# Fewer picked columns on ScalarE, addresses loaded behind each operation, window sums placed ahead of the edge network

## The chip, the core and the metric

The kernel runs on one core of a Trainium2 chip. The core has a matrix engine (TensorE, PE in the profile; its weight loads are shown apart as PEld), a vector engine (VectorE, DVE), an activation engine (ScalarE, ACT), GpSimd (POOL) and a queue engine (SyncE, SP) that here only starts DMA transfers. Each engine executes its own instruction stream in order; they wait for one another through semaphores. The metric is the device time of one execution in microseconds; the median of several runs is compared.

## What is computed

One layer of a graph network on 12,500 nodes with 128 features and 412,500 edges, sorted by destination. The 128 features are 32 scalars and 32 vectors of three components. For each edge:

```python
h   = gelu(gelu(edge_attr_8 @ W_mlp1 / sqrt(8)) @ W_mlp2 / sqrt(64))
w00, w01, w10, w11 = h @ Wp_00, h @ Wp_01, h @ Wp_10, h @ Wp_11
e0, e1 = feat0[src], feat1[src]            # rows gathered at the edge's source node
mid0 = [w00*e0*a0,  w11*sum(e1*a1)/sqrt3]  # a0, a1: edge_attr_4
mid1 = [w01*e0*a1,  w10*e1*a0]
n0, n1 = segment_sum(mid0, dst), segment_sum(mid1, dst)
```

The sums go through two small matrices, are mixed with a linear map of the node itself, and the result plus the input x is normalised over its 128 features. `feat0, feat1` are x times a 128x128 matrix `wf`.

## The kernel before, in words

**Tiling.** A run is 512 consecutive edges (128 partitions x Q = 4 columns). There are 806 runs, handled two at a time: NP = 403 pairs, the trips of the main loop (`for p in range(NP)`, unrolled). Two pairs make a chunk of four runs: the pair with k = 0 is called the even pair here, that with k = 1 the odd pair. A first phase (some 190 us) turns x into the transposed copy `xT` that stays in SBUF, and into a table of features in DRAM.

**Where an edge's features come from.** For a run, 4 x 128 rows of 512 bytes are needed in the tile `G`. There are three ways to get a quarter of a run (128 rows):

- GpSimd gathers it from the table by an indirect DMA (`gather`, line 223 of the profile), about 18 runs ahead, into one of ten buffers.
- SP copies the rows of every fourteenth run one by one with plain DMAs whose addresses it reads from a list (`aid`, line 208).
- VectorE or ScalarE picks it: it copies 128 columns of `xT` one at a time into a tile `gt` (lines 188 and 192), each from an address held in a register; TensorE then multiplies the tile by `wf` (line 197) and ScalarE copies the product into `G` (line 198, `picked_rows`). The registers are filled by an instruction that loads addresses from an SBUF list (line 174). A quarter that is picked isn't gathered.

How many columns are picked in a pair, and where between other operations, is set by the table `SLOTS`: on ScalarE four slots a pair, 12, 16, 16 and 12 columns, from pair FROM = 6 on. With 397 pairs that fills 171 tiles of 128.

**The order within a pair.** The order of each engine's instructions is the order in which the loop body emits them (a manual schedule); buffers and semaphores alone decide when one may start. In the loop body, for pair p of chunk c:

1. gather for a later pair (POOL), loads of edges (SP).
2. even pair: VectorE makes `pl` (`placing`, L683) and `oh` (`hot_rows`, L624), both of which read constants kept in the PSUM tile `bank`.
3. TensorE sums the messages of pair p-1 into windows of nodes (`segments`, L670, tile `seg`); ScalarE copies the window to SBUF (`segments_kept`, L676, tile `sg`) within slot 0.
4. `picked_rows`; odd pair: `radial` (transposes edge attributes for a chunk ahead, L543/L545).
5. ScalarE slot 1; TensorE `weights(p+1)` (L597).
6. the edge network two chunks ahead: in the even pair `mlp1` (L554) with its two gelus (`gelu1`, L559), in the odd pair `mlp2` (L570) with `gelu2` (L576). The gelus stand within ScalarE's slots 2 and 3.
7. even pair: ScalarE copies edge attributes into `bank` (`show`, L632), between the two gelus.
8. even pair: TensorE adds the four window sums of the chunk before to one PSUM tile at offsets read from registers (`place`: a zeroing matmul L693 and eight matmul passes L697), which is again `bank`.
9. VectorE: three operations of `messages` (L650, L654 twice) with its own slots of picked columns between them; in the odd pair `select` (L639, tile `S`), which reads `bank`, and `add` (L710), which adds the placed sums to the accumulator `acc`.

`bank` is one PSUM tile with three uses: the placed sums, the shown attributes, and the constants. The framework that sets the waits orders accesses to a tile by the order in which the loop body emits them.

**A slot with an operation.** `picks` loads part of the slot's addresses ahead of the operation (`fetch(e, n // 8 * 4)`: 4 of 12, 8 of 16), issues the operation, loads the rest, and copies all columns of the slot.

Of the kernel before, what the change touches and what calls it, by code (L numbers as in the profile page):

```python
# [8 lines left out]
F32 = mybir.dt.float32  # L9
# [6 lines left out]
ACT = mybir.EngineType.Activation  # L16
DVE = mybir.EngineType.DVE
# [4 lines left out]
P = 128  # L22
# [7 lines left out]
CH = 4  # L30
PR = 2
# [14 lines left out]
AID_FROM = 36  # L46
AID_LEAD = 16
STEPS = 12
SLOTS = {DVE: ((24, 20, 20), (24, 16, 28)), ACT: ((12, 16, 16, 12), (12, 16, 16, 12))}
FROM = {DVE: 6, ACT: 6}  # L50
COL_Q = {DVE: Q - 2, ACT: Q - 3}
A_OF = (1, 2, 3, 0)
# [5 lines left out]
def gnn_kernel(ctx: ExitStack, tc: tile.TileContext, x, src, dst, ea4, ea8, w1_0, w1_1, wm1, wm2,  # L58
# [33 lines left out]
    x_bytes = xT.bitcast(U8)  # L92
    x_bytes = bass.AP(tensor=x_bytes.tensor, offset=x_bytes.offset - x_at, ap=[[4 * N, P], [1, x_at + 4 * N]])
# [18 lines left out]

    per_chunk = {e: sum(map(sum, slots)) for e, slots in SLOTS.items()}
    picked = {}
    for e, slots in SLOTS.items():
        picked[e], done = [], 0
# [46 lines left out]

    taken = {e: 0 for e in picked}

    def fetch(e, n):

        at = taken[e]
        n = min(n, len(picked[e]) * P - at)
        if n <= 0:  # L170
            return []
        taken[e] += n
        row, c0 = divmod(at, per_chunk[e])
        _, r = nc.values_load_multi_w_load_instructions(  # L174
            pick_rows[e, row // P][row % P:row % P + 1, c0:c0 + n], engines=[e], min_val=x_at,
            max_val=x_at + 4 * (N - 1), skip_runtime_bounds_check_because="addresses of columns")
        return [(at + k, r[k]) for k in range(n)]

    def copy_columns(e, columns):

        for at, r in columns:
            i, j = divmod(at, P)
            if j == 0:
                GT[e, i] = wk.tile([P, P], F32, name=f"gt{list(picked).index(e)}", bufs=3)
            to = GT[e, i][:, j:j + 1]
            col = x_bytes[:, bass.ds(r.with_bounds(guaranteed_mod_val=0, out_of_modulus=4), 4)].bitcast(F32)
            if e == DVE:
                nc.vector.tensor_copy(to, col)  # L188
                if waiting and j % 2:
                    waiting.pop(0)()  # L190
            else:
                nc.scalar.activation(to, col, AF.Copy)  # L192
# [192 lines left out]
    for b in range(NG):  # L385
        c = math.ceil((min((b + 1) * GN, N) + MARGIN) / N * NCH) - 1
# [202 lines left out]
    def weights(p):  # L589

        c, k = divmod(p, CH // PR)
        runs = [i for i in range(PR) if p * PR + i < NS]
        WP[p] = ps.tile([P, PR, Q, P], F32, name="w")
        for q in range(Q):
            for i in runs:
                rows = slice(i * HID, (i + 1) * HID)
                nc.tensor.matmul(WP[p][:, i, q, :], H2[c][q % 2][rows, k, q // 2, :], wpb[rows, :],  # L597
                                 start=True, stop=True)
# [29 lines left out]
    def show(c):  # L628

        n = min(CH, NS - c * CH)  # L630
        t0 = c * CH % ET * Q
        nc.scalar.activation(shown[:, :, :n * Q], e4[c * CH // ET][:, :, t0:t0 + n * Q], AF.Copy)  # L632
# [40 lines left out]
    def segments_kept(p):  # L673
        c, r = divmod(p * PR, CH)
        n = min(PR, NS - p * PR)
        nc.scalar.activation(SG[c][:, r:r + n, :], SEG[c][:, r:r + n, :], AF.Copy)  # L676
# [9 lines left out]
    def place(c):  # L686
        ns = min(CH, NS - c * CH)
        b, r = divmod(c, P)
        _, at = nc.values_load_multi_w_load_instructions(
            run_first[b][r:r + 1, :], engines=[PE], min_val=0, max_val=4 * (SPAN - W),  # L690
            skip_runtime_bounds_check_because="bounded above")
        ST[c] = pt = bank[:, :4 * SPAN].rearrange("p (a n) -> p a n", a=4)
        nc.tensor.matmul(pt.rearrange("p a n -> p (a n)"), none[:, :P], none, start=True, stop=False)  # L693
        to = pt.bitcast(U8)
        for k in range(ns):
            k_at = at[k].with_bounds(guaranteed_mod_val=0, out_of_modulus=4)
            nc.tensor.matmul(to[:, :, bass.ds(k_at, 4 * W)].bitcast(F32), SG[c][:, k, :],  # L697
                             PL[c][:, k, :].rearrange("p (a n) -> p a n", a=4), start=False, stop=k == ns - 1)
# [54 lines left out]
    waiting = []  # L753
# [188 lines left out]
    with tc.manual_schedule(engines={PE, ACT, DVE, SP}):  # L942
# [54 lines left out]
        clearing = []  # L997
        placed = added = 0

        def picks(e, p, i, op=None):  # L1000
            if p < FROM[e]:
                if op:
                    op()
                return
            n = SLOTS[e][p % (CH // PR)][i]
            if not op:
                copy_columns(e, fetch(e, n))
                return
            first = fetch(e, n // 8 * 4)
            op()  # L1010
            copy_columns(e, first + fetch(e, n - n // 8 * 4))

        for p in range(NP):
            c, k = divmod(p, CH // PR)
            mine = [s for s in range(p * PR, (p + 1) * PR) if s < NS]
            if p:
                for s in mine:
                    if s + LEAD - PR < NS:
                        gather(s + LEAD - PR)
            if k == 1 and c + EDGES_AHEAD < NCH:  # L1020
                load_edges(c + EDGES_AHEAD)
            for s in mine:
                if s % P == P // 2 - 16 and (s // P + 1) * P < NS:
                    load_raws(s // P + 1)
                if s % P == P // 2 and (s // P + 1) * P < NS:
                    load_indices(s // P + 1)
                if s % ET == 8 and s - 8 + ET < NS:
                    load_attributes(s // ET + 1)
                for t in range(P // ROWS):
                    a = s + AID_LEAD - t * STEPS // (P // ROWS)  # L1030
                    if a in aided:
                        aid(a, t)
            nets = c + 2 < NCH
            if k == 0:
                placing(c)
                if c + 1 < NCH:
                    hot_rows(c + 1)
            if p:
                segments(p - 1)
                picks(ACT, p, 0, lambda: segments_kept(p - 1))  # L1040
            for e in picked:
                for s in mine:
                    if (e, s + 2 * PR) in pick_of:
                        picked_rows(e, pick_of[e, s + 2 * PR])
            if k == 1 and c + 3 < NCH:
                radial(c + 3)
            cleared = bool(late)
            rest = list(kept)
            norm_kept()
            picks(ACT, p, 1)  # L1050
            if p + 1 < NP:
                weights(p + 1)
            if nets:
                (mlp1, mlp2)[k](c + 2)
                picks(ACT, p, 2, lambda: (gelu1, gelu2)[k](c + 2, 0))
            else:
                picks(ACT, p, 2)
            if k == 0 and c + 1 < NCH:
                show(c + 1)
            for s in mine:  # L1060
                if s % ET == 20 and s - 20 + ET < NS:
                    turn_attributes(s // ET + 1)
            if nets:
                picks(ACT, p, 3, lambda: (gelu1, gelu2)[k](c + 2, 1))
            else:
                picks(ACT, p, 3)
            if k == 0 and c > 0:
                place(c - 1)
                placed = c
            raws_next = [s + PR for s in mine if s + PR < raw_runs]  # L1070
            for s in raws_next:
                turn_rows(s)
            messages(p, 0)
            if k == 0:
                picks(DVE, p, 0)
            messages(p, 1)
            picks(DVE, p, 1 - k)
            for s in raws_next:
                features(s)
            if rest:  # L1080
                norm_rest()
            if cleared:
                new_sums()
                clearing += list(range(4))
            elif clearing:
                clear_sums(clearing.pop(0))
            if k == 1 and c + 1 < NCH:
                select(c + 1)
            if k == 1:
                picks(DVE, p, 1)  # L1090
            messages(p, 2)
            if k == 1 and placed > added:
                add(added)
                added += 1
            picks(DVE, p, 2)
            if k == 0 and 0 < added == c - 1:
                norm(due.get(added - 1, []))
            if p == 0:
                addresses()
                find_first()  # L1100
                new_sums()
                clearing = list(range(4))
            if p == NP - 4:
                count_odd()
# [52 lines left out]
```

## Time and profile before

| what | value |
|---|---|
| median of 3 runs | 5994.51 us (5955.32 to 5994.96) |
| the profiled execution | 5962.68 us, span 5960.8 us |
| instructions | 141,936 |
| busy share of the span: PE, PEld | 57 %, 44 % |
| DVE, ACT, POOL | 56 %, 52 %, 44 % |
| clock granted to TensorE, mean | 0.65 of full speed |
| DMA | 40 GB/s, busy 1 to 2 tenths |

Busy counts neither the loading of registers nor the issuing of DMAs. All five engines lie between 44 and 57 percent, so no share names the limit; the idle time and what ends it has to be read. "Idle before" in a group of instructions is the time in which the engine stood still just before one of the group; behind the arrow stands what ended most of it, "issue" where the profile shows no cause and "remote" where it shows no instruction that did it.

### The profile page before, as it was taken

What the parts mean: (1) busy time and instruction counts of PE and PEld (TensorE: products, weight loads), DVE (VectorE), ACT (ScalarE), POOL (GpSimd) and SP (SyncE); (2) the same over time, 40 slices, a digit from 0 to 9 for tenths busy, and PEclk for the clock granted to TensorE, in tenths of its full rate; (3) what the DMA queues carried; (4) which work ended last, traced back from release to release, by engine and by line L of the source; (5) the groups of instructions that cost most, each with busy time, mean ns of one, the idle gap of its engine ahead of it and who ended that gap; (6) DMA issues with size and microseconds to landing.
All of it is one profiled execution on the core that took longest, in us unless ns stands there. A gap on an engine that the chain in (4) does not pass through costs nothing. (4 is left out here: it accounts for less than half of the span.)

```text
span 5960.8 us, 141936 instructions
## 1 busy us (share of the span) xinstructions
PE 3407.7 (57%) x30231; PEld 2603.1 (44%) x30231; DVE 3366.2 (56%) x28706; ACT 3093.4 (52%) x24111; POOL 2636.3 (44%) x2801
## 2 busy tenths in 40 slices
PE   3665655556555555555556555556655555655556
PEld 2544444444444444444444444444434444443444
DVE  1265656555655555656555665566565555665556
ACT  0254555555555555555555555555554555555554
POOL 4344444444444444444444444444444444444441
PEclk5766666666666666666666666666666666666666
DMA  4211111111111111111111111111111111111111
GB/s 100 59 36 40 39 35 38 41 35 43 42 35 39 39 37 43 40 35 36 36 41 37 40 43 38 37 40 40 41 40 35 35 38 38 40 40 34 40 33 23
DMA packets 576979, 239.04 MB, mean 40 GB/s; under 512 B 481402, under 2 KB 526570, under 8 KB 576106
## 3 DMA queue, kind: packets, MB, share of 16 engines
q0 software_dynamic: 89408, 183.29, 10.8%
q1 hardware_dynamic: 465928, 40.14, 5.4%
q10 hardware_dynamic: 20770, 6.47, 0.5%
q14 instruction: 629, 5.15, 0.3%
q8 instruction: 244, 4.00, 0.3%
HBM read 216.86 MB, written 12.99 MB: 39 GB/s over the span
## 5 line engine op out<-in xcount | busy, mean ns | idle before, releaser
L223 POOL DMA_INDIRECT G<-table,idx x2722 | 2567.2, 943 | 3208.9 <-issue 1313.3
L192 ACT ACTIVATE gt<-xT 128x1 f32 x21888 | 2329.1, 189 | 924.5 <-issue 889.3
L188 DVE COPY gt<-xT 128x1 f32 x25984 | 1891.8, 145 | 1565.0 <-issue 1520.5
L670 PE MATMUL seg<-M,S 128*32 128x128 f32 x12896 | 845.7, 371 | 444.2 <-issue 426.8
L597 PE MATMUL w<-wpb,h 64*128 64x128 f32 x6448 | 855.1, 388 | 383.7 <-issue 383.1
L597 PEld LDWEIGHTS w<-wpb,h 64*128 64x128 f32 x6448 | 699.0, 277 | 554.6 <-issue 544.1
L670 PEld LDWEIGHTS seg<-M,S 128*32 128x32 f32 x12896 | 544.3, 148 | 692.1 <-issue 643.3
L654 DVE TENSOR_TENSOR M<-w,G 128x768 f32<-128x768 f32 x806 | 761.1, 945 | 2.7 <-issue 2.7
L676 ACT ACTIVATE sg<-seg 128x256 f32<-128x256 f32 x403 | 151.1, 375 | 1112.3 <-remote 777.6
L697 PEld LDWEIGHTS m<-pl,sg 128*128 128x128 f32 x1612 | 348.6, 312 | 797.7 <-issue 797.7
L693 PE MATMUL m<-none 128*128 128x384 bf16 x202 | 90.8, 450 | 786.1 <-ACT m L632 412.6
L554 PE MATMUL h<-eT,w1b 64*128 64x128 f32 x3232 | 439.3, 403 | 125.8 <-ACT G L198 95.9
L576 ACT ACTIVATE h<-h 128x512 f32<-128x512 f32 x404 | 237.1, 589 | 491.9 <-remote 377.0
L554 PEld LDWEIGHTS h<-eT,w1b 64*128 64x128 f32 x3232 | 394.3, 303 | 159.5 <-ACT G L198 120.5
L570 PE MATMUL h<-h,w2b 64*64 64x256 f32 x3232 | 393.5, 556 | 105.7 <-ACT G L198 68.7
L197 PE MATMUL h<-wf,gt 128*128 128x128 f32 x748 | 244.0, 411 | 268.2 <-issue 154.2
L650 DVE TENSOR_TENSOR M<-w,G 128x512 f32<-128x512 f32 x403 | 275.5, 684 | 204.1 <-remote 73.9
L697 PE MATMUL m<-pl,sg 128*128 128x128 f32 x1612 | 367.5, 404 | 0.0
L197 PEld LDWEIGHTS h<-wf,gt 128*128 128x128 f32 x748 | 162.8, 263 | 403.6 <-issue 246.9
L639 DVE TENSOR_TENSOR S<-oh,m 128x512 f32<-128x512 f32 x202 | 137.2, 679 | 356.7 <-PE m L697 251.4
L559 ACT ACTIVATE h<-h 128x512 f32<-128x512 f32 x404 | 234.6, 581 | 91.0 <-remote 37.9
L570 PEld LDWEIGHTS h<-h,w2b 64*64 64x64 f32 x3232 | 187.5, 186 | 214.9 <-ACT G L198 87.3
(123 smaller groups left out, 1592.5 us busy)
## 6 DMA issues: line engine op xcount, KB each, us to landing
G<-table SPq DMA_DIRECT2D x7040, 0.5 KB
G<-table,idx POOLq DMA_INDIRECT x2722
e<-in_edge_attr SPq DMA_DIRECT2D x201, 64.0 KB
xt<-in_x SPq DMA_DIRECT2D x24, 256.0 KB
table<-ft ACTq DMA_DIRECT2D x24, 256.0 KB
xt<-in_edge_attr SPq DMA_DIRECT2D x24, 256.0 KB
out<-y SPq DMA_DIRECT2D x24, 256.0 KB
xt<-in_dst SPq DMA_DIRECT2D x5, 256.0 KB
```

The source lines that it names most:

```text
L188: nc.vector.tensor_copy(to, col)
L192: nc.scalar.activation(to, col, AF.Copy)
L197: nc.tensor.matmul(pt, GT.pop((e, i)), wf, start=True, stop=True)
L223: nc.gpsimd.indirect_dma_start(out=G[s][:, q, :], out_offset=None, in_=x if s < raw_runs else table, in_offset=bass.IndirectOffsetOnAxis(a ...
L554: nc.tensor.matmul(p1[h][:, j // 2, j % 2, :], w1b[rows, j, :], eT[c][rows, :], start=True, stop=True)
L570: nc.tensor.matmul(p2[r][k * HID:(k + 1) * HID, h * n:(h + 1) * n], w2b[rows, :], H1[c][h][rows, k * n:(k + 1) * n], start=True, stop=True)
L576: nc.scalar.activation(H2[c][r].rearrange("p k j e -> p (k j e)"), P2[c][r], AF.Gelu_apprx_tanh, scale=1.0 / math.sqrt(HID))
L597: nc.tensor.matmul(WP[p][:, i, q, :], H2[c][q % 2][rows, k, q // 2, :], wpb[rows, :], start=True, stop=True)
L650: nc.vector.tensor_tensor(m[:, :, :, :MUL], w[:, :, :2 * MUL].rearrange("p q (a u) -> p q a u", a=2), g[:, :, None, :MUL].to_broadcast([P, ...
L654: nc.vector.tensor_tensor(m[:, :, j, MUL:].rearrange("p q (i u) -> p q i u", i=3), w[:, :, None, (2 + j) * MUL:(3 + j) * MUL].to_broadcast ...
L670: nc.tensor.matmul(SEG[c][q * W:(q + 1) * W, r + i, :], own[:, (r + i) * Q + q, h * W:(h + 1) * W], M[p][:, i, q, h, :], start=h == 0, sto ...
L697: nc.tensor.matmul(to[:, :, bass.ds(k_at, 4 * W)].bitcast(F32), SG[c][:, k, :], PL[c][:, k, :].rearrange("p (a n) -> p a n", a=4), start=F ...
```

## The change

Three things change, all within the main loop:

- ScalarE's slots become 12, 12, 12 and 8 columns (44 a pair in place of 56). What ScalarE no longer picks is gathered by GpSimd.
- A slot's addresses are loaded at once, with one instruction, behind the operation in front of it. `fetch` and `copy_columns` become one function, `pick`; `segments_kept` and the gelus stand ahead of the slot whose middle they were in. The second gelu now stands ahead of `turn_attributes`.
- `place` moves from the end of TensorE's even pair to between `weights(p+1)` and `mlp1`, so ahead of `show` too. Lines behind the first edit have numbers four lower in the changed kernel (L670 becomes L666).

VectorE's slots stay; only where the small steps of the normalisation are put between its columns follows a column's place in the slot rather than in the tile.

```diff
-SLOTS = {DVE: ((24, 20, 20), (24, 16, 28)), ACT: ((12, 16, 16, 12), (12, 16, 16, 12))}
+SLOTS = {DVE: ((24, 20, 20), (24, 16, 28)), ACT: ((12, 12, 12, 8), (12, 12, 12, 8))}
...
-    def fetch(e, n):
+    def pick(e, n):
...
-        return [(at + k, r[k]) for k in range(n)]
-
-    def copy_columns(e, columns):
-
-        for at, r in columns:
-            i, j = divmod(at, P)
+        for k in range(n):
+            i, j = divmod(at + k, P)
...
-                if waiting and j % 2:
+                if waiting and k % 2:
                     waiting.pop(0)()
...
-        def picks(e, p, i, op=None):
-            if p < FROM[e]:
-                if op:
-                    op()
-                return
-            n = SLOTS[e][p % (CH // PR)][i]
-            if not op:
-                copy_columns(e, fetch(e, n))
-                return
-            first = fetch(e, n // 8 * 4)
-            op()
-            copy_columns(e, first + fetch(e, n - n // 8 * 4))
+        def picks(e, p, i):
+            if p >= FROM[e]:
+                pick(e, SLOTS[e][p % (CH // PR)][i])
...
             if p:
                 segments(p - 1)
-                picks(ACT, p, 0, lambda: segments_kept(p - 1))
+                segments_kept(p - 1)
+            picks(ACT, p, 0)
...
             picks(ACT, p, 1)
             if p + 1 < NP:
                 weights(p + 1)
+            if k == 0 and c > 0:
+                place(c - 1)
+                placed = c
             if nets:
                 (mlp1, mlp2)[k](c + 2)
-                picks(ACT, p, 2, lambda: (gelu1, gelu2)[k](c + 2, 0))
-            else:
-                picks(ACT, p, 2)
+                (gelu1, gelu2)[k](c + 2, 0)
+            picks(ACT, p, 2)
             if k == 0 and c + 1 < NCH:
                 show(c + 1)
+            if nets:
+                (gelu1, gelu2)[k](c + 2, 1)
             for s in mine:
                 if s % ET == 20 and s - 20 + ET < NS:
                     turn_attributes(s // ET + 1)
-            if nets:
-                picks(ACT, p, 3, lambda: (gelu1, gelu2)[k](c + 2, 1))
-            else:
-                picks(ACT, p, 3)
-            if k == 0 and c > 0:
-                place(c - 1)
-                placed = c
+            picks(ACT, p, 3)
```

More of the change, by code (lines that the diff above doesn't have):

```diff
@@ L170, in fetch @@
         if n <= 0:
-            return []
+            return
         taken[e] += n
@@ L185, in copy_columns @@
             to = GT[e, i][:, j:j + 1]
-            col = x_bytes[:, bass.ds(r.with_bounds(guaranteed_mod_val=0, out_of_modulus=4), 4)].bitcast(F32)
+            col = x_bytes[:, bass.ds(r[k].with_bounds(guaranteed_mod_val=0, out_of_modulus=4), 4)].bitcast(F32)
             if e == DVE:
                 nc.vector.tensor_copy(to, col)
-                if waiting and j % 2:
+                if waiting and k % 2:
                     waiting.pop(0)()
```

## The prediction

> **What bounds the kernel now.** The page came first: its groups of instructions, with the idle time before each.
>
> ```profile
> L223 POOL DMA_INDIRECT G<-table,idx x2722 | 2567.2, 943 | 3208.9 <-issue 1313.3
> L192 ACT ACTIVATE gt<-xT 128x1 f32 x21888 | 2329.1, 189 | 924.5 <-issue 889.3
> L188 DVE COPY gt<-xT 128x1 f32 x25984 | 1891.8, 145 | 1565.0 <-issue 1520.5
> L676 ACT ACTIVATE sg<-seg 128x256 f32<-128x256 f32 x403 | 151.1, 375 | 1112.3 <-remote 777.6
> L693 PE MATMUL m<-none 128*128 128x384 bf16 x202 | 90.8, 450 | 786.1 <-ACT m L632 412.6
> L576 ACT ACTIVATE h<-h 128x512 f32<-128x512 f32 x404 | 237.1, 589 | 491.9 <-remote 377.0
> L559 ACT ACTIVATE h<-h 128x512 f32<-128x512 f32 x404 | 234.6, 581 | 91.0 <-remote 37.9
> L639 DVE TENSOR_TENSOR S<-oh,m 128x512 f32<-128x512 f32 x202 | 137.2, 679 | 356.7 <-PE m L697 251.4
> ```
>
> Three waits form a ring. TensorE stands 786 us in front of `place` (L693), mostly until ScalarE's `show` (L632) has written the shared tile. ScalarE stands 1112 us in front of the window copy L676, for TensorE's sums. VectorE stands 357 us in front of `select` (L639), for `place`. ScalarE hardly waits at the first gelu (91 us). Next, the chain of waits, asked for 4400 to 5900 us, then rows of the waits (us, times, longest) and of single lines (shortest/median/longest in ns, first and last start):
>
> ```profile
> by line: ACT gt L192 24.6%; another core or an unknown queue 21.6%; issue 15.6%; ACTq L174 4.5%; PE seg L670 4.1%; PE m L697 3.4%; DVE gt L188 3.0%; ACT h L576 3.0%; PE h L570 2.4%; ACT h L559 2.2%; PE w L597 2.0%; PE h L554 2.0%; ACT sg L6
> ...
> DVE S L639 <- PE m L697: 251.4, 69, 9.3
> DVE acc L710 <- ACT acc L428: 169.6, 15, 18.2
> DVE S L639 <- remote: 67.4, 14, 7.1
> ...
> L676 ACT ACTIVATE sg<-seg x403: 357/383/385, 209.7 to 5938.6; 128x256 f32<-128x256 f32 x135
> ...
> L174 ACTq TENSOR_LOAD <-pick x2736: 305/552/1912, 279.9 to 5901.4; - x196
> ```
>
> ScalarE's picked columns are a quarter of the chain, VectorE's 3%: the ring of ScalarE and TensorE sets the pace, and VectorE follows. L676 gives the period: (5938.6 - 209.7) / 402 = 14.25 us a pair. Last, the timeline of one even pair and the start of the odd one, engine by engine (start, duration, instructions, in brackets the idle time before):
>
> ```profile
> 3008.28 0.38 ACT L676 ACTIVATE sg<-seg 128x256 f32<-128x256 f32 x1 [0.20 <-remote]
> 3008.93 1.22 ACT L192 ACTIVATE gt<-xT 128x1 f32 x12 [0.27 <-issue]
> 3010.16 0.28 ACT L198 ACTIVATE G<-h 128x128 f32<-128x128 f32 x1
> 3011.31 1.59 ACT L192 ACTIVATE gt<-xT 128x1 f32 x16 [0.87 <-issue]
> 3012.81 0.57 ACT L559 ACTIVATE h<-h 128x512 f32<-128x512 f32 x1
> 3013.28 1.58 ACT L192 ACTIVATE gt<-xT 128x1 f32 x16
> 3014.76 0.21 ACT L632 ACTIVATE m<-e 128x64 f32<-128x64 f32 x1
> ...
> 3018.05 0.30 ACT L192 ACTIVATE gt<-xT 128x1 f32 x2 [1.12 <-issue]
> 3019.47 0.30 ACT L192 ACTIVATE gt<-xT 128x1 f32 x2 [1.13 <-issue]
> ...
> 3022.79 0.38 ACT L676 ACTIVATE sg<-seg 128x256 f32<-128x256 f32 x1 [0.96 <-PE h L543]
> ...
> 3027.72 0.60 ACT L576 ACTIVATE h<-h 128x512 f32<-128x512 f32 x1 [0.92 <-PE h L570]
> 3028.37 1.59 ACT L192 ACTIVATE gt<-xT 128x1 f32 x16
> 3029.87 0.58 ACT L576 ACTIVATE h<-h 128x512 f32<-128x512 f32 x1
> ```
>
> ```profile
> 3010.49 2.07 PE L554 MATMUL h<-eT,w1b 64*128 64x128 f32 x14 [0.55 <-ACT G L198]
> 3016.70 0.48 PE L693 MATMUL m<-none 128*128 128x384 bf16 x1 [4.13 <-ACT h L559]
> 3016.97 1.91 PE L697 MATMUL m<-pl,sg 128*128 128x128 f32 x8
> 3018.81 1.94 PE L670 MATMUL seg<-M,S 128*32 128x128 f32 x32
> 3020.67 0.80 PE L197 MATMUL h<-wf,gt 128*128 128x128 f32 x2
> 3022.65 2.08 PE L597 MATMUL w<-wpb,h 64*128 64x128 f32 x16
> 3024.88 1.71 PE L570 MATMUL h<-h,w2b 64*64 64x256 f32 x16
> ```
>
> ```profile
> 3018.06 0.21 DVE L188 COPY gt<-xT 128x1 f32 x2 [1.21 <-issue]
> 3019.48 0.22 DVE L188 COPY gt<-xT 128x1 f32 x2 [1.20 <-PE m L697]
> ...
> 3012.34 0.94 POOL L223 DMA_INDIRECT G<-table,idx  x1 [6.04 <-issue]
> 3013.58 0.94 POOL L223 DMA_INDIRECT G<-table,idx  x1 [0.30 <-issue]
> 3019.83 0.94 POOL L223 DMA_INDIRECT G<-table,idx  x1 [0.30 <-issue]
> ```
>
> ScalarE and VectorE resume at the same instants, 3018.05 and 3019.47: both freeze together, between short bursts of two columns, and this stands in the later part of POOL's burst of seven gathers (3012.34 to 3020.77). I call this the frozen stretch. From the end of `show` (3014.97) to the next copy (3022.79) pass 7.8 us, in which ScalarE has a gelu (0.57) and twelve columns (1.22) to do: 6.0 of this pair's 14.5 us are frozen, as an estimate; "issue" before VectorE's columns, 1520 us, bounds it for the span at a quarter. No engine's work explains it.
>
> **The change part by part.** The sum starts from the profiled execution, 5962.7 us, which lies 0.5% below the median of the runs, 5994.5; what the launch adds to the span (1.9 us) stays. All path sums below are without frozen time.
>
> *Columns.* The changed program picks 17,280 columns on ScalarE in place of 21,888: 4608 fewer, at (1.59 - 1.22) / 4 = 0.093 us each, 1.11 us a pair and 426 us of ScalarE in all.
>
> *Address loads.* 1571 in place of 2736. The gaps price them: eight addresses behind the copy L676 (0.38) leave 0.27, so 0.65 from its start; sixteen behind L198 (0.28) leave 0.87, so 1.15; hence 0.0625 an address, 0.90 for twelve. Gaps then: 0.52 behind L676, 0.62 behind L198, 0.33 behind the first gelu (0.57), 0.08 for eight behind the second: 1.55 a pair. Before: 0.27 + 0.87 = 1.14, and up to 0.92 more where a load stands in front of a gelu that was ready (3027.72: the matmuls ended at 3026.59). That is -0.9 to +0.4 us a pair, 360 us less to 160 more. I take the change as inside the paths below. [...]
>
> *Even pair, window copy to window copy.* Now: ScalarE to the end of `show` 6.69 us (3008.28 to 3014.97), `place` 2.18, sums 1.87: 10.7. After: `place` waits for the window copy, which is its input, and not for `show`. If TensorE is ahead, as at 3022.79, where the sums ended 2.04 us before the copy: 0.38 + 2.18 + `mlp1` 2.37 (14 passes in 2.07, 16 wanted) = 4.93, then gelu 0.57, gap 0.33, twelve columns 1.22, `show` 0.21, gelu 0.57, gap 0.08, eight columns 0.85: 8.8, 2.0 less. If TensorE is not ahead: 0.80 (L197) + 2.08 (L597) + 2.18 + 2.37 = 7.43, with the same rest 11.3: 0.5 more. I take the first, the row that this trace has.
>
> *Odd pair.* Now 4.93 us from copy to first gelu2 and 2.15 more to the second. After: 0.38 + 0.52 + 1.22 + 0.28 + 0.25 (a second small copy) + 0.62 + 1.22 = 4.49, with the matmuls ready 3.80 behind the copy; 0.57 + 0.33 + 1.22 = 2.12 to the second gelu; and behind it four columns fewer, 0.37: 0.8 less together.
>
> So a chunk loses 2.8 us or, with the other even pair, 0.3. Over 199 chunks: 550 or 50 us.
>
> *What is late next.* VectorE, whose work stays. It can gain only its waits: 319 us before `select` and, as ScalarE moves the accumulator earlier, perhaps half of the 170 before L710: 404. A third of that I put to the frozen stretch, which lies between the quarter and the 6.0 of 14.5 above. That leaves **269 us**, the smaller of the two limits, and it is the term I take. The new wait of `place` for VectorE's last reads of the tile (`placing` and `hot_rows`) holds up `mlp1` and the moments behind it; VectorE does both at the start of its even pair, so I put it at nothing.
>
> *Gathers.* 36 more on POOL. Lower bound nothing: POOL rests 6.04 us between bursts. Upper: 1.25 us each plus its share of the frozen stretch, 6.0 / 7 = 0.86: 76 us. I take the upper end, since the row next to it is the frozen one.
>
> Sum: 5962.7 - 269 + 76 = **5770**.
>
> **The rivals.** *Fewer instructions, shorter freeze.* If the freeze begins after so many instructions of a burst, 14.5 fewer of 352 a pair (141,936 / 403) shorten it: 8.5 us unfrozen in that pair, 41 instructions a microsecond, 0.35 us a pair, 139 us more than forecast: 5630. For it: every engine stops at once. Against: no row shows what fills. [...]
>
> *The gain doesn't arrive.* TensorE is free earlier but waits at the sums for VectorE's messages, or `place` waits for ScalarE all the same, through the window copy. Then the odd pair's 0.8 x 199 x 2/3 = 106 us less 76 remain: 5933, spreading to the unchanged time.
>
> *Slower: `place` on the way to the gelu.* The 786 us at L693 may be time that TensorE had to spare. Then 2.18 us of `place` now stand between ScalarE's copy and its first gelu, where ScalarE waits almost never today (91 us). It decides when TensorE is not ahead at the even copy: ScalarE's own way to the gelu is 4.2 us (0.38 + 0.52 + 1.22 + 0.28 + 0.62 + 1.22), TensorE's 7.43, so it waits 3 us a chunk and the dropped columns buy nothing. Price: 0.5 x 199 x 2/3 = 67, the odd pair gains nothing, gathers 76: 6106; with cheaper gathers 6030.
>
> **How the numbers follow.** Forecast 5770 (5660 to 5900) 0.47; shorter freeze 0.08; the gain doesn't arrive 0.13; slower 0.32. A measurement of this kernel can tell about 1% from no change. Faster 0.55, same 0.13, slower 0.32. The range goes from 5640, inside the shorter freeze's case, to 6090, inside the slower one's; the forecast's own range stands beside it.
>
> **What would show it.** Right: L689 (`place`) idle far below 786 us; VectorE's wait at `select` below 100; ScalarE's at the window copy about halved; the chain moved from ScalarE's columns to VectorE's columns, loads and messages; period near 13.8 us. Slower rival: idle before the gelu L555 from 91 to over 400 us, and the period above 14.3. Gathers: longer bursts, with frozen rows over more of each pair. The forecast is wrong if VectorE's waits stay although `place` is early, or if its freed time comes back as "issue".

## The result

The changed kernel takes 5809.6 us (median of 4, 5786.8 to 5821.8), the kernel before 5985.1 on the same chip: a ratio of 0.971, 95% interval 0.966 to 0.976. The forecast was 5770, in a range from 5640 to 6090. The profiled execution took 5812.9 us, 150 less than the profiled one of before; the forecast's sum had 193.

Of the profile after, first the groups of instructions that answer to those of before (line numbers four lower; behind the bar busy time, mean of one in ns, and the idle time before them with what ended it):

```profile
L219 POOL DMA_INDIRECT G<-table,idx x2758 | 2601.8, 943 | 3025.8 <-issue 1293.0 <-ACT gt L188 545.9 <-DVE M L650 502.4
L184 DVE COPY gt<-xT 128x1 f32 x25984 | 1905.6, 145 | 1662.8 <-issue 1625.5 <-DMA G<-table,idx 8.7 <-remote 1.1
L188 ACT ACTIVATE gt<-xT 128x1 f32 x17280 | 1790.0, 189 | 425.2 <-issue 408.2 <-DMA G<-table 0.7
L572 ACT ACTIVATE h<-h 128x512 f32<-128x512 f32 x404 | 237.6, 589 | 586.4 <-remote 449.8 <-PE h L566 116.9 <-issue 14.1
L555 ACT ACTIVATE h<-h 128x512 f32<-128x512 f32 x404 | 236.7, 587 | 437.0 <-PE h L550 228.3 <-remote 198.9 <-issue 7.4
L672 ACT ACTIVATE sg<-seg 128x256 f32<-128x256 f32 x403 | 152.6, 379 | 1501.1 <-remote 1107.4 <-PE seg L666 158.6 <-PE h L193 113.5
L635 DVE TENSOR_TENSOR S<-oh,m 128x512 f32<-128x512 f32 x202 | 136.4, 675 | 143.7 <-ACT m L628 79.5 <-issue 48.7 <-ACT gt L188 7.7
L706 DVE TENSOR_TENSOR acc<-m,acc 128x384 f32 x202 | 110.9, 549 | 180.8 <-ACT acc L424 134.9 <-ACT y L737 39.0 <-issue 5.5
L689 PE MATMUL m<-none 128*128 128x384 bf16 x202 | 94.6, 468 | 48.0 <-remote 35.6 <-DVE oh L620 5.3 <-DVE acc L706 4.8
```

The wait in front of `place` is gone (786 to 48 us), and VectorE's in front of `select` with it (357 to 144). Two waits have grown. ScalarE now stands 437 us in front of the first layer's gelus, which had been 91, and 1501 in front of the window copy, which had been 1112. VectorE's idle time without a cause, before its columns, has grown from 1520 to 1625 us. Then the timeline of one even pair of the changed kernel, ScalarE first, TensorE behind it:

```profile
3020.53 0.38 ACT L672 ACTIVATE sg<-seg 128x256 f32<-128x256 f32 x1 [2.42 <-remote]
3021.40 1.22 ACT L188 ACTIVATE gt<-xT 128x1 f32 x12 [0.48 <-issue]
3022.52 0.26 ACT L194 ACTIVATE G<-h 128x128 f32<-128x128 f32 x1
3022.92 1.22 ACT L188 ACTIVATE gt<-xT 128x1 f32 x12
3025.29 0.60 ACT L555 ACTIVATE h<-h 128x512 f32<-128x512 f32 x1 [1.15 <-PE h L550]
3026.16 1.22 ACT L188 ACTIVATE gt<-xT 128x1 f32 x12 [0.28 <-issue]
3027.29 0.20 ACT L628 ACTIVATE m<-e 128x64 f32<-128x64 f32 x1
3027.44 0.58 ACT L555 ACTIVATE h<-h 128x512 f32<-128x512 f32 x1
3027.91 0.84 ACT L188 ACTIVATE gt<-xT 128x1 f32 x8
```

```profile
3015.82 0.27 PE L666 MATMUL seg<-M,S 128*32 128x128 f32 x1 [1.17 <-issue]
3017.23 0.37 PE L193 MATMUL h<-wf,gt 128*128 128x128 f32 x1 [1.15 <-issue]
3018.66 0.37 PE L193 MATMUL h<-wf,gt 128*128 128x128 f32 x1 [1.05 <-issue]
3020.06 2.13 PE L593 MATMUL w<-wpb,h 64*128 64x128 f32 x16 [1.03 <-issue]
3022.13 0.50 PE L689 MATMUL m<-none 128*128 128x384 bf16 x1
3022.42 1.66 PE L693 MATMUL m<-pl,sg 128*128 128x128 f32 x8
3024.01 1.16 PE L550 MATMUL h<-eT,w1b 64*128 64x128 f32 x16
```

`place` (L689, L693) follows the weights without a gap, and the gelu starts 4.76 us behind the window copy; ScalarE waited 1.15 for it. From the copy to the end of the last column pass 8.2 us; the forecast had 4.9 and 8.8. The window copy itself starts at 3020.53, though the sums that it copies (L666) ended at 3016.09: between them TensorE starts one instruction every 1.4 us, the step at which VectorE and ScalarE resume in the forecast's frozen stretch (3018.05 and 3019.47). So the 1501 us in front of the copies hold frozen time too, and not only a wait for sums.

### The profile page after: what moved, and what is told of

Its sections match the earlier page's. It is cut to its first block, busy times and chain, and to the rows that moved or that the text cites. A ratio compares the mean times of both kernels' runs of the same rounds, so it can differ in the third digit from the quotient of the medians.

```text
span 5811.1 us, 135970 instructions
## 1 busy us (share of the span) xinstructions
PE 3376.4 (58%) x30159; PEld 2478.4 (43%) x30159; DVE 3372.9 (58%) x28706; ACT 2580.9 (44%) x19467; POOL 2670.8 (46%) x2837
## 5 line engine op out<-in xcount | busy, mean ns | idle before, releaser
L219 POOL DMA_INDIRECT G<-table,idx x2758 | 2601.8, 943 | 3025.8 <-issue 1293.0
L188 ACT ACTIVATE gt<-xT 128x1 f32 x17280 | 1790.0, 189 | 425.2 <-issue 408.2
L666 PE MATMUL seg<-M,S 128*32 128x128 f32 x12896 | 843.3, 342 | 661.4 <-issue 532.5
L593 PE MATMUL w<-wpb,h 64*128 64x128 f32 x6448 | 887.0, 405 | 365.9 <-issue 365.2
L593 PEld LDWEIGHTS w<-wpb,h 64*128 64x128 f32 x6448 | 732.8, 293 | 555.5 <-issue 545.3
L666 PEld LDWEIGHTS seg<-M,S 128*32 128x32 f32 x12896 | 506.0, 135 | 945.1 <-issue 758.0
L672 ACT ACTIVATE sg<-seg 128x256 f32<-128x256 f32 x403 | 152.6, 379 | 1501.1 <-remote 1107.4
L650 DVE TENSOR_TENSOR M<-w,G 128x768 f32<-128x768 f32 x806 | 761.1, 945 | 1.9 <-issue 1.9
L566 PE MATMUL h<-h,w2b 64*64 64x256 f32 x3232 | 454.0, 617 | 376.6 <-ACT G L194 213.4
L693 PEld LDWEIGHTS m<-pl,sg 128*128 128x128 f32 x1612 | 337.2, 291 | 110.8 <-issue 76.0
L693 PE MATMUL m<-pl,sg 128*128 128x128 f32 x1612 | 342.9, 378 | 54.7 <-ACT sg L672 29.3
L550 PE MATMUL h<-eT,w1b 64*128 64x128 f32 x3232 | 313.8, 336 | 44.7 <-issue 19.7
L550 PEld LDWEIGHTS h<-eT,w1b 64*128 64x128 f32 x3232 | 264.8, 235 | 86.7 <-issue 46.2
L539 PE MATMUL h<-ident,e 128*128 128x128 f32 x202 | 78.2, 387 | 286.9 <-ACT G L194 172.5
```

The costliest lines, as they stand in the source:

```text
L219: nc.gpsimd.indirect_dma_start(out=G[s][:, q, :], out_offset=None, in_=x if s < raw_runs else table, in_offset=bass.IndirectOffsetOnAxis(a ...
L550: nc.tensor.matmul(p1[h][:, j // 2, j % 2, :], w1b[rows, j, :], eT[c][rows, :], start=True, stop=True)
L566: nc.tensor.matmul(p2[r][k * HID:(k + 1) * HID, h * n:(h + 1) * n], w2b[rows, :], H1[c][h][rows, k * n:(k + 1) * n], start=True, stop=True)
L650: nc.vector.tensor_tensor(m[:, :, j, MUL:].rearrange("p q (i u) -> p q i u", i=3), w[:, :, None, (2 + j) * MUL:(3 + j) * MUL].to_broadcast ...
L666: nc.tensor.matmul(SEG[c][q * W:(q + 1) * W, r + i, :], own[:, (r + i) * Q + q, h * W:(h + 1) * W], M[p][:, i, q, h, :], start=h == 0, sto ...
```

## The experiments

The kernels of a set ran on one chip beside the kernel before; the ratios are to that kernel in the same set.

### One part at a time

*Place alone.* `place` stands between `weights` and the network layer; columns and loads stay.

```diff
             if p + 1 < NP:
                 weights(p + 1)
+            if k == 0 and c > 0:
+                place(c - 1)
+                placed = c
             if nets:
...
-            if k == 0 and c > 0:
-                place(c - 1)
-                placed = c
             raws_next = [s + PR for s in mine if s + PR < raw_runs]
```

> Only the placed sums move ahead of the network layer; 56 columns and the split loads stay. Ring theory: the even pair loses the wait for show; what is left of it is ScalarE's own 9.4 us in place of 10.7, so 1.3 x 199 x 2/3 = 170 us less, ratio about 0.97, and VectorE's wait at select falls from 357 to under 150 us. Column theory (ScalarE's load alone is the limit): ScalarE has as much to do and now waits for mlp1 too, ratio 1.00 to 1.02. Either way the idle time in front of the placing matmul falls below 100 us.

Measured: 5915.4 us, ratio 0.987 (0.984 to 0.990). From its groups:

```profile
L559 ACT ACTIVATE h<-h 128x512 f32<-128x512 f32 x404 | 236.7, 586 | 540.8 <-remote 356.9 <-PE h L554 149.0 <-issue 31.1
L676 ACT ACTIVATE sg<-seg 128x256 f32<-128x256 f32 x403 | 150.8, 374 | 605.2 <-remote 454.9 <-PE seg L670 108.9 <-PE w L597 26.7
L639 DVE TENSOR_TENSOR S<-oh,m 128x512 f32<-128x512 f32 x202 | 136.4, 675 | 347.6 <-ACT m L632 188.5 <-remote 82.8 <-ACT h L559 47.7
L693 PE MATMUL m<-none 128*128 128x384 bf16 x202 | 95.5, 473 | 25.4 <-remote 14.7 <-DVE acc L710 4.8 <-issue 3.0
```

The wait in front of `place` goes (786 to 25 us), but VectorE's at `select` does not: 348 us, now for ScalarE's `show` itself in place of the `place` behind it. With 56 columns ScalarE is late either way. The 77 us gained are less than half of the 170 that the ring theory gave.

*Columns alone.*

```diff
-SLOTS = {DVE: ((24, 20, 20), (24, 16, 28)), ACT: ((12, 16, 16, 12), (12, 16, 16, 12))}
+SLOTS = {DVE: ((24, 20, 20), (24, 16, 28)), ACT: ((12, 12, 12, 8), (12, 12, 12, 8))}
```

> Only 44 columns in place of 56; place stays late and the loads stay split. Ring theory: show comes 8 columns earlier (0.74 us) and the odd pair ends 0.8 us earlier, 1.54 x 199 x 2/3 = 204 us less, 36 gathers give 76 back: ratio 0.98. Place theory (all of the gain is the wait for show): the gathers alone remain, ratio 1.01. The idle time in front of place stays above 600 us either way.

Measured: 5805.6 us, ratio 0.968 (0.965 to 0.971).

```profile
L676 ACT ACTIVATE sg<-seg 128x256 f32<-128x256 f32 x403 | 153.2, 380 | 2020.2 <-remote 1450.6 <-PE seg L670 314.2 <-PE h L197 131.6
L639 DVE TENSOR_TENSOR S<-oh,m 128x512 f32<-128x512 f32 x202 | 136.6, 676 | 128.8 <-PE m L697 61.7 <-issue 54.7 <-remote 11.3
L710 DVE TENSOR_TENSOR acc<-m,acc 128x384 f32 x202 | 110.8, 548 | 104.9 <-ACT acc L428 46.8 <-ACT y L741 33.5 <-issue 23.2
L650 DVE TENSOR_TENSOR M<-w,G 128x512 f32<-128x512 f32 x403 | 275.1, 683 | 218.1 <-remote 117.2 <-ACT G L615 72.2 <-issue 17.9
L693 PE MATMUL m<-none 128*128 128x384 bf16 x202 | 86.8, 429 | 485.2 <-ACT m L632 248.0 <-ACT gt L192 90.6 <-remote 48.7
```

This one line is worth as much as the whole change, and more than the 0.98 of the ring theory. `place` still waits 485 us for `show`, less than the 600 expected, and VectorE's wait at `select` has fallen to 129 us all the same. ScalarE now seems to come early enough for both.

*Loads alone.*

```diff
-            first = fetch(e, n // 8 * 4)
             op()
-            copy_columns(e, first + fetch(e, n - n // 8 * 4))
+            copy_columns(e, fetch(e, n))
```

> Only the loads: all addresses of a slot behind its operation, 56 columns, place late. By the gaps of the profile the loads of a pair change by -0.9 to +0.4 us of ScalarE: ratio 0.98 to 1.02, middle 1.00. A theory in which the loads ahead of the operation cost (a ready gelu waits behind them) says 0.98; one in which they hide a wait says 1.01 to 1.02.

Measured: 6044.2 us, ratio 1.008 (1.005 to 1.011).

```profile
L192 ACT ACTIVATE gt<-xT 128x1 f32 x21888 | 2328.5, 189 | 1143.2 <-issue 1124.3
```

The idle time without a cause before ScalarE's columns rises from 889 to 1124 us. The likely reading, which no run separates: longer loads now stand in the open behind the operations, and a load ahead of an operation no longer uses the time in which ScalarE waits for its input.

*All but the place.* The changed kernel with `place` back behind `show`.

```diff
             if p + 1 < NP:
                 weights(p + 1)
-            if k == 0 and c > 0:
-                place(c - 1)
-                placed = c
...
             picks(ACT, p, 3)
+            if k == 0 and c > 0:
+                place(c - 1)
+                placed = c
```

> The changed kernel with place put back behind the network layer and show: 44 columns and loads at once stay. Ring theory: half of the gain goes, ratio to the kernel before 0.98 to 0.99, with over 600 us idle in front of place and over 250 us at select. Column theory: as fast as the changed kernel, 0.97. Place theory: no faster than before, 1.00 to 1.01.

Measured: 5819.2 us, ratio 0.971 (0.967 to 0.974): what the changed kernel has.

```profile
L635 DVE TENSOR_TENSOR S<-oh,m 128x512 f32<-128x512 f32 x202 | 136.3, 675 | 132.4 <-PE m L693 68.2 <-issue 46.4 <-remote 16.5
L689 PE MATMUL m<-none 128*128 128x384 bf16 x202 | 89.2, 441 | 496.5 <-ACT m L628 257.4 <-issue 113.6 <-ACT gt L188 69.2
```

`place` waits 497 us again, and `select` no longer than in the changed kernel. So the early place, worth 1.3% with 56 columns, is worth nothing with 44: in the time of the kernel the three parts don't add up. One account is that the first and the second take away the same lateness of ScalarE; the count of frozen time further down speaks for another.

### What is the limit with 44 columns

*Fewer columns on VectorE.* On top of the columns alone:

```diff
-SLOTS = {DVE: ((24, 20, 20), (24, 16, 28)), ACT: ((12, 12, 12, 8), (12, 12, 12, 8))}
+SLOTS = {DVE: ((16, 16, 16), (16, 12, 20)), ACT: ((12, 12, 12, 8), (12, 12, 12, 8))}
```

> Base: the kernel before with 44 columns on ScalarE (slots_only, 0.968). VectorE's slots shrink to 48 columns a pair (from 64 and 68), 56 more gathers. Theory that VectorE has become the limit: 18 columns a pair at 0.06 us, 1.09 x 397 x 2/3 = 288 us less, 56 gathers at 2.1 us give 118 back: ratio 0.94. Theory that the frozen stretch, and so the count of gathers, is the limit: 118 us more, ratio 0.99.

Measured: 6111.2 us, ratio 1.021 (1.018 to 1.023), slower than either theory.

```profile
L188 DVE COPY gt<-xT 128x1 f32 x18816 | 1370.1, 147 | 901.4 <-issue 891.7 <-DMA G<-table,idx 4.8
L639 DVE TENSOR_TENSOR S<-oh,m 128x512 f32<-128x512 f32 x202 | 137.5, 681 | 1180.2 <-PE m L697 969.3 <-remote 193.4 <-issue 17.2
L693 PE MATMUL m<-none 128*128 128x384 bf16 x202 | 91.9, 455 | 1008.4 <-ACT m L632 619.1 <-ACT h L559 158.4 <-remote 146.9
```

VectorE did get early, and then stood 1180 us in front of `select`, for a `place` that itself waited 1008 us, mostly for `show`. So fewer columns on VectorE don't help this version, and the ring through TensorE and ScalarE is back. It has `place` late, so it doesn't test VectorE as the limit of the changed kernel. Why it takes longer than with VectorE's full slots is taken up with the frozen time below.

*Fewer columns still on ScalarE.*

```diff
-SLOTS = {DVE: ((24, 20, 20), (24, 16, 28)), ACT: ((12, 12, 12, 8), (12, 12, 12, 8))}
+SLOTS = {DVE: ((24, 20, 20), (24, 16, 28)), ACT: ((8, 8, 8, 8), (8, 8, 8, 8))}
```

> Base slots_only again, with 32 columns a pair on ScalarE (8 in each slot), 37 more gathers. Theory that VectorE is the limit at 44 columns: ScalarE's relief buys nothing, the gathers cost 0 to 78 us, ratio 0.968 to 0.981. Theory that ScalarE's columns still set the pace: another 150 to 200 us less, minus the gathers, 0.95.

Measured: 5735.5 us, ratio 0.957 (0.954 to 0.959), 1.5% below the changed kernel by the ratios; of the versions run on the chips of the first two sets that compute the whole layer this is the fastest.

```profile
L676 ACT ACTIVATE sg<-seg 128x256 f32<-128x256 f32 x403 | 153.9, 382 | 2620.2 <-remote 1980.4 <-PE seg L670 322.6 <-PE h L197 181.1
L639 DVE TENSOR_TENSOR S<-oh,m 128x512 f32<-128x512 f32 x202 | 136.0, 673 | 49.2 <-issue 47.1 <-remote 0.8 <-PE m L697 0.6
L710 DVE TENSOR_TENSOR acc<-m,acc 128x384 f32 x202 | 111.2, 550 | 75.4 <-ACT acc L428 34.0 <-ACT y L741 31.9 <-issue 8.1
L650 DVE TENSOR_TENSOR M<-w,G 128x512 f32<-128x512 f32 x403 | 276.0, 685 | 115.2 <-ACT G L615 79.6 <-issue 24.5 <-DMA G<-table,idx 2.6
L693 PE MATMUL m<-none 128*128 128x384 bf16 x202 | 86.3, 427 | 283.1 <-ACT m L632 233.5 <-ACT gt L192 26.7 <-ACT h L559 12.4
```

ScalarE stands still in front of the window copy for almost half of the span (frozen time included), and dropping more of its columns still pays, in spite of 37 more gathers: the waits for it, at `select` (129 to 49 us) and at `place` (485 to 283), go on falling. VectorE's waits at `select`, the accumulator (L710) and the first operation of `messages` (L650) fall together from 452 to 240 us, and its idle time put to "issue" before its columns rises from 1648.8 to 1804.5.

### The price of a gather, and the frozen stretch

*One more gather a pair*, in 394 pairs, in the changed kernel:

```diff
+            if s >= raw_runs and s % PR == 0 and q == 0:
+                spare = wk.tile([P, P], F32, name="spare", bufs=2)
+                nc.gpsimd.indirect_dma_start(
+                    out=spare, out_offset=None, in_=table,
+                    in_offset=bass.IndirectOffsetOnAxis(ap=rows, axis=0))
```

> The changed kernel with one more indirect gather in each of 394 pairs, into a spare tile that nothing reads. It prices a gather: 2.1 us each, as in the forecast's sum, gives 830 us, ratio to the kernel before 1.11; hidden beside other work, 0.97; 1.25 us each (the time of the instruction alone), 1.05.

Measured: 6333.1 us, ratio 1.056 (1.053 to 1.059). Against the changed kernel's 0.971 that is 0.085 of the 6000 us of the kernel before in this set, 508 us, or 1.29 us a gather; the 36 of the change then cost about 46 us. By the medians of the two sets it is 1.33. That is no less than the 1.25 from one gather to the next in a burst, so GpSimd's rest between bursts seems to hide none of it; 104 us of GpSimd's waiting in this run was for the spare tile's own two buffers, which a gather of the change doesn't have, so the price is rather an upper one.

*Plain transfers in place of gathers*, from the same queue, of as many rows:

```diff
-            nc.gpsimd.indirect_dma_start(
-                out=G[s][:, q, :], out_offset=None, in_=x if s < raw_runs else table,
-                in_offset=bass.IndirectOffsetOnAxis(ap=rows, axis=0))
+            if s < raw_runs:
...
+            else:
+                nc.gpsimd.dma_start(G[s][:, q, :], table[(s % 96) * P:(s % 96 + 1) * P, :])
```

> The changed kernel with each indirect gather of the main loop replaced by a plain transfer of 128 consecutive rows of the table from the same GpSimd queue; this leaves the gathering by source node out. If the indirect gathers make the frozen stretches, the idle time put to issue before VectorE's columns falls from 1626 us towards the loads of addresses alone, some 500 us, and the time by about a quarter to a fifth. If the frozen stretches come with the number of instructions, both stay within 3%.

Measured: 3649.2 us, ratio 0.609 (0.607 to 0.611). The busy shares of its page, and two groups:

```profile
PE 2491.4 (68%) x30159; PEld 1898.2 (52%) x30159; DVE 3149.4 (86%) x28706; ACT 2502.2 (69%) x19467; POOL 1522.6 (42%) x2837
...
L184 DVE COPY gt<-xT 128x1 f32 x25984 | 1702.9, 146 | 215.6 <-issue 189.5
L224 POOL DMA_DIRECT2D G<-table x2758 | 1453.5, 535 | 2015.6 <-issue 606.0 <-DVE M L653 527.2 <-ACT h L558 393.0
```

The same 2758 transfers of 64 KB, 135,975 instructions in place of 135,970 and 578,125 DMA packets in place of 578,124. The idle time without a cause falls from 1625 to 190 us, and VectorE is busy for 86% of the span. With the indirect gathers the frozen stretches are gone too, and the kernel is 2160 us shorter, more than the 1520 us of "issue" that bounded the stretches in the forecast. A count of instructions or packets alone doesn't make them. Not all of the 2160 us need be freezing: the granted clock is 0.824 here and 0.676 in the changed kernel, and TensorE is busy for 2491 us in place of 3376. Which of the two follows from the other no run shows.

*The frozen time counted.* The idle time put to "issue" misses what freezes during a wait. The traces allow a direct count: the sum of all stretches of over 0.35 us in which neither TensorE (weight loads included) nor VectorE nor ScalarE starts an instruction, from 200 us on to 30 us before the end. It holds some common waiting too; the plain transfers and the last row, with only 190 and 193 us put to "issue" before VectorE's columns, show how much: 272 and 219 us.

| kernel | span, us | without a start | the rest |
|---|---|---|---|
| before | 5961 | 1696 | 4265 |
| place alone | 5909 | 1979 | 3930 |
| columns alone | 5796 | 1745 | 4051 |
| loads alone | 6058 | 1743 | 4315 |
| all but the place | 5811 | 1677 | 4134 |
| changed | 5811 | 1938 | 3873 |
| columns alone, fewer on VectorE | 6078 | 2208 | 3870 |
| columns alone, 32 on ScalarE | 5740 | 2055 | 3685 |
| changed, one more gather a pair | 6337 | 2437 | 3900 |
| changed, plain transfers | 3652 | 272 | 3380 |
| columns and place, other chip | 3587 | 219 | 3368 |

The early place makes the rest 335 us shorter with 56 columns and 261 with 44, and the time without a start 283 and 261 longer. (With 0.55 us for 0.35 the two increases are 219 and 223.) So what it saves comes back as time in which nothing starts. That time grows within GpSimd's bursts, from 1173 us with `place` late to 1435 with it early, and between them stays the same (468 and 467). The same holds for fewer columns on VectorE: the rest falls by 181 us and the time without a start rises by 463. These are one trace each. Whether the freeze grows because the engines get ahead, or only fills what some other limit leaves free, no run shows.

### A set on a chip without frozen stretches

The last four kernels ran on another chip, on which the kernel before takes 3879 us (median of 7, 3872 to 3888), not 5985 to 6000; their ratios are comparable among themselves, not with those above.

*Columns and place, split loads* (the two diffs above together):

> The kernel before with 44 columns and place early; the loads stay split. It completes the table of the three parts. If the early place is worth its 1.3% with 44 columns too: 0.956 of the kernel before. If TensorE's wait for show is spare time at 44 columns, as late_place (0.971) beside the changed kernel (0.971) says: 0.968, as slots_only.

Measured: 3585.8 us, ratio 0.924 (0.922 to 0.927), below both theories, which were made for the chips that freeze; so it doesn't complete the table of the three parts. Three groups:

```profile
L223 POOL DMA_INDIRECT G<-table,idx x2758 | 2603.3, 944 | 862.0 <-issue 752.6 <-DMA G<-table,idx 55.2 <-DVE M L654 9.5
L188 DVE COPY gt<-xT 128x1 f32 x25984 | 1702.8, 144 | 218.8 <-issue 193.4
L639 DVE TENSOR_TENSOR S<-oh,m 128x512 f32<-128x512 f32 x202 | 134.2, 664 | 0.0
```

The gathers are there, 944 ns each as before, and the idle time without a cause is 193 us. With no frozen stretch GpSimd becomes a limit: 2603 busy and 862 idle, the latter 0.31 us between gather and gather, fill 3465 of 3587 us. VectorE stands close beside it, busy for 88% of the span.

*The same with fewer columns on VectorE* (SLOTS of VectorE as in the run with fewer columns on VectorE):

> split_early with VectorE's 48 columns a pair of dve_less. dve_less was slow (1.02) with 1180 us of VectorE in front of select, for a place that waited for show. If that ring is what made it slow, the early place takes the wait to under 300 us and the ratio to 0.93 to 0.97. If the frozen stretches of 56 more gathers are what made it slow, it stays at 1.00 to 1.02.

Measured: 3645.0 us, ratio 0.940 (0.938 to 0.942), slower than with VectorE's full slots.

```profile
L639 DVE TENSOR_TENSOR S<-oh,m 128x512 f32<-128x512 f32 x202 | 134.2, 664 | 2.8 <-ACT m L632 2.6
L650 DVE TENSOR_TENSOR M<-w,G 128x512 f32<-128x512 f32 x403 | 277.8, 689 | 705.1 <-DMA G<-table,idx 396.0 <-PE w L597 53.3 <-DMA G<-table 46.6
```

There is no wait at `select`, but on this chip there was none with VectorE's full slots either (0.0), so it says nothing for the ring theory. VectorE now waits 396 us for gathers to land: the 56 more, at 1.25 us, are 70 us of a busy GpSimd, and 59 us is what the kernel lost. It doesn't tell what held the run on the other chip.

*20 columns on ScalarE* (8, 4, 4, 4; place late):

> slots_only with 20 columns a pair on ScalarE (8, 4, 4, 4) after 32 gave 0.957. 37 more gathers at the 1.33 us that extra_gather measured: 49 us. If ScalarE's columns still cost their chain: another 50 to 70 us less net, 0.945. If VectorE is the limit: 49 us more, 0.965.

Measured: 3670.0 us, ratio 0.946 (0.944 to 0.948). Here 74 more gathers than in the run with 44 columns stand beside 84 us more. That the ratio is the 0.945 of the first theory is chance: that number was worked out for the other chips. The run can't tell whether the way from 44 to 32 columns goes on, since here GpSimd is a limit (2673.5 us busy and 873.6 idle, of 3669.6).

*Gathers of consecutive rows*, in the changed kernel:

```diff
-            rows = idx_raw[:, s, q:q + 1] if s < raw_runs else idx[b][:, q, c:c + 1]
+            rows = idx_raw[:, s, q:q + 1] if s < raw_runs else in_order[:, s % 96:s % 96 + 1]
```

> The changed kernel with indirect gathers as before, but with a fixed list of consecutive rows (the rows that plain_pool read) in place of the source nodes; gathering by source node is left out. If scattered rows in DRAM make the frozen stretches, the time falls to near plain_pool's 0.61. If the indirect instruction does, it stays at 0.96 to 0.98.

Measured: 3588.2 us, ratio 0.925 (0.922 to 0.928). With the same number of gathers it takes as long as the columns and place above (3585.8). On a chip that doesn't freeze (190.7 us put to "issue" before VectorE's columns) it says nothing of freezing, and the question that it was made for is open: whether the indirect instruction or its scattered rows freeze the engines.

## Why the prediction was right, and where it was not

**The sign and the size** came out: 150 us less in the profiled execution where the sum had 193. Its terms were less right than its total.

**Ring theory.** Right in its core: the kernel before is paced by ScalarE and TensorE waiting for each other, and ScalarE's columns are on that path. The columns alone (0.968) show it; in the count above they make the rest of the span 214 us shorter and the time without a start only 49 longer. The wait at `select` fell to 144 us, not below 100 as the forecast wanted. The chain moved part of the way: ScalarE's columns make 11.2% of it in place of 24.6, VectorE's 9.7% in place of 3.0 (in the stretch from 5230 to 5780 us after, 4400 to 5900 before).

**Even pair.** The forecast chose the case in which TensorE is ahead, 8.8 us from copy to last column; the timeline after shows 8.2, and 4.76 to the gelu for the 4.93 forecast. The agreement is partly luck. The forecast had TensorE free at the copy; in the timeline it was in the middle of the weights, so `place` started 1.60 us behind the copy's start and not 0.38, and `mlp1` took 1.3 us to the gelu and not 2.37. The step also credited the gain to the moved `place`, and there it failed: with the columns cut, the kernel takes as long with `place` early or late (0.971 and 0.971). The slower rival said that the wait of `place` was spare time; by the count above the early place does shorten the rest of the span, by 261 us, and time without a start takes 261 back. The path sums were "without frozen time", and a third off the cap was all that the forecast left for it.

**Slower rival.** Its mechanism is there: ScalarE's wait at the first layer's gelus rose to 437 us, beyond the 400 that was to show it, and to 541 with the place alone. It doesn't decide: the period did not rise above 14.3 us, and even with 56 columns the early place gained 1.3%.

**Address loads** were taken as nothing within -360 and +160 us. The lower end doesn't follow from its terms: 1.55 - 1.14 - 0.92 is -0.5 us a pair, some 205 us. (Nor is 0.3 us in 199 chunks 50 us, but 60; neither enters the forecast.) Alone the loads cost 52 us (0.8%). With 44 columns late_place and the columns alone differ by 14 us, and their intervals overlap. The shortest load with the columns alone took 0.304 us, in the changed kernel, with a slot's loads at once, 0.541.

**Gathers** were oversized: 76 us at 2.1 each, against 1.29 measured, 46. Bursts didn't grow longer, as the forecast had it (6.8 gathers each before and after, counting those less than 1.5 us apart as one); per burst more time passes without a start, 4.8 us in place of 4.3 (1938 us over 401 bursts, 1696 over 398).

**What is late next.** This step was the weakest. The forecast took VectorE's waits as what can be gained, 404 us of them, and left a third of that to the frozen stretch. The waits did fall, by 213 us at `select` and 28 at the accumulator, 241 together. But 105 us came back as "issue", the sign that the forecast had named for being wrong: that is 44% of what was gained, not a third. So both numbers of the term were off, 241 us in place of 404 and 44% in place of a third, and the frozen time did not stay what it was: 1938 us without a start after, 1696 before. What is left of the waits, 136 us, has the price of the gathers in it already; the forecast had 269 and took 76 off. That its 193 came near the 150 measured is luck in part, since too large a gain and too dear a gather partly offset each other. Whether VectorE is the next limit stays open. With 32 columns on ScalarE the kernel got faster, and it is again VectorE's waits that fell (452 to 240 us). Fewer columns on VectorE made it slower (1.021), but with `place` late. What does bound the kernel at 44 columns, on the chips that freeze, is not settled beyond this: each gather at its full price, ScalarE's columns, and the time without a start, which grew by 242 us while the rest fell by 392.

**ScalarE's wait for the sums** was to be halved and rose to 1501 us. ScalarE, with 4608 columns fewer, stood there 389 us longer, and part of that idle time is frozen; halving was a slip of reasoning. The period of 13.89 us, (5788.2 - 203.0) / 402 from the first and last start of L672, is close to the 13.8 given:

```profile
L672 ACT ACTIVATE sg<-seg x403: 357/383/385, 203.0 to 5788.2; 128x256 f32<-128x256 f32 x135
```

**Shorter freeze.** The rival wanted 5630 us from 4% fewer instructions, and the changed kernel lies 180 above it. The run with fewer columns on VectorE, 129,444 instructions to the 137,118 of the columns alone, took longer by 5%. The time without a start got longer with the change (1696 to 1938 us), not shorter. With plain transfers 272 us without a start are left, at 37 instructions and 158 DMA packets a microsecond in place of 23 and 99, so neither count nor rate is a cause by itself; what starts a freeze within a burst no run shows. All executions here have the profiler's records (each has its granted clock), so no run shows either whether the freeze is there without them.

## What to carry to other kernels

A wait of 786 us on one engine gave 77 us with the early place alone and nothing with 44 columns: it is worth only what the ring around it can give back, and the gains of two edits need not add up. Try each alone and each left out, and count in each trace how long no engine starts anything, since time saved in one place can come back there, as 261 us did here. Work moved off an engine that stands still can still pay, if it stands in front of what another engine waits for: ScalarE stood 2020 of 5796 us in front of the window copy with 44 columns, and with 12 columns fewer the ratio went from 0.968 to 0.957. Where all engines stand still at the same instants, as for most of the 1938 us without a start in the changed kernel, look for the transfer that runs then, and replace it by a plain one to price it: here that left 272 us.

## What had not been expected

- With indirect gathers all engines freeze together on the chip of the second set: with as many plain transfers from the same queue the kernel takes 3649 us, 0.609 of the kernel before, where the changed kernel has 0.971; the time without a start is 272 us, where the other kernels of the set have 2055 to 2437. The chip of the first set shows the same stretches (1677 to 1979 us without a start); there no plain transfers were run. The gather itself lasts 0.94 us in either surrounding, so its own row shows nothing.
- The same kernel takes 3879 us on a chip without the frozen stretches, with 0.77 of the TensorE clock granted where the others had 0.65. There GpSimd is a limit (2603 us busy and 862 idle, of 3587): 20 columns on ScalarE with `place` late, so 74 more gathers, stand beside 84 us more, where on the chips that freeze 37 more gathers for 12 columns left the kernel faster (0.957 after 0.968). Columns and place take 0.924 of the kernel before there, where the changed kernel has 0.971 on the others. What sets the chips, or the two sessions, apart no run shows.
- Loads of more addresses took longer: those of 4 0.32 us, of 12 0.79 us, as the median durations of the columns-alone run and the changed kernel say:

```profile
L174 ACTq TENSOR_LOAD <-pick x2749: 304/320/2043, 284.6 to 5747.2; - x197
```

```profile
L174 ACTq TENSOR_LOAD <-pick x1571: 541/788/1590, 282.6 to 5764.9; - x197
```
